# Where a graph kernel's adjacency is normalised: raw transposes with sums from their evacuations, against sums and scaling first

## The chip, the cores and the metric

The kernel runs on one core of one Trainium2 chip. The time is device microseconds of one execution, and each kernel is quoted by the median of its fast runs. Ratios are the mean time of one kernel's fast runs over that of the other's in the same rounds, so they are not quite the ratio of the medians quoted beside them. A difference under 2% is called "same".

## The reference, cut to what matters

```python
A_norm = A + jnp.eye(n)                                  # n = 1024
deg = jnp.sum(A_norm, axis=0) + jnp.sum(A_norm, axis=1) - jnp.diagonal(A_norm)
dinv = jax.lax.rsqrt(deg)
A_hat = A_norm * dinv[:, None] * dinv[None, :]
agg = jnp.einsum('nm,bmd->bnd', A_hat, features)         # 16 batches, d = 256
# then: linear, batch norm, relu, linear, batch norm, residual, layer norm,
# and a second layer with attention over 1024 nodes; none of that is changed
```

Everything after `agg` needs the normalised adjacency. It is computed once, at the start.

## The kernel before

All data is fp32. The adjacency arrives as four transfers of two row tiles each (a row tile is 128 rows by 1024). TensorE contracts over partitions, so the aggregation wants the adjacency transposed (`AhT`).

```python
            for i in range(NT):                                  # NT = 8 row tiles
                blk = A[i][:, ts(i, P)]
                nc.vector.tensor_add(blk, blk, ident)
                nc.vector.tensor_reduce(deg[:, i : i + 1], A[i], AX.X, OP.add)
                nc.vector.scalar_tensor_tensor(scr, blk, 1.0, ident, ..., accum_out=diag[:, i : i + 1])
            # [cut: W1 and W2 transposed on TensorE, evacuated by ScalarE]
            pd = ps.tile([P, FB], F32, tag="a", name="pd")
            for j in range(NT):
                for i in range(NT):                              # column sums: ones as moving operand
                    nc.tensor.matmul(pd[:, j : j + 1], A[i][:, ts(j, P)], ones, start=(i == 0), stop=(i == NT - 1))
            # [cut: deg = row sums + pd - diag; dinv = deg ** -0.5 on GpSimd]
            for i in range(NT):
                nc.vector.tensor_scalar_mul(A[i], A[i], dinv[:, i : i + 1])
            for j in range(NT):
                for h in range(NH):                              # NH = 2 halves of 512 nodes
                    p = ps.tile([P, FB], F32, tag="a", name="pat")
                    for k in range(FB // P):
                        nc.tensor.transpose(p[:, ts(k, P)], A[h * 4 + k][:, ts(j, P)], ident)
                    # [cut] evacuated times dinv of j, by VectorE (odd h) or ScalarE (even h)
```

In these traces each engine works in the order of the program text, on its own. In the aggregation one batch is four groups (two channel halves `c`, two node halves `h`) of eight accumulating matmuls. The trace shows every fp32 matmul as two records, so one batch is 64 records.

Of the kernel before, what the change touches and what calls it, by code (L numbers as in the profile page):

```python
# [9 lines left out]
F32 = mybir.dt.float32  # L10
AF = mybir.ActivationFunctionType
OP = mybir.AluOpType
AX = mybir.AxisListType
# [3 lines left out]
P = 128  # L17
# [5 lines left out]
def gnn_norm_attention_kernel(  # L23
# [16 lines left out]
    nc = tc.nc  # L40
    B, N, C = x.shape
    H = W1.shape[0]
    NT = N // P
    CT = C // P
    HT = H // P
    FB = 512
    NH = N // FB
# [7 lines left out]
    ident = const.tile([P, P], F32, name="ident")  # L55
    make_identity(nc, ident)
    ones = const.tile([P, 1], F32, name="ones")
# [4 lines left out]
    def rsqrt(dst, src, add):  # L62

        n = src.shape[1]
        if add:
            nc.gpsimd.tensor_scalar(dst, src, add, None, op0=OP.add)  # L66
            src = dst
        nc.gpsimd.tensor_tensor(dst, src, mhalf[:, :n], OP.pow)  # L68


    def load_vec(src, n, name):
        t = const.tile([P, n], F32, name=name)
        with nc.allow_non_contiguous_dma(reason="a few hundred numbers"):
            nc.sync.dma_start(t, src.rearrange("(c p) -> p c", p=P))
        return t
# [10 lines left out]
    with ExitStack() as l0:  # L86
        w0 = l0.enter_context(tc.tile_pool(name="w0", bufs=1))
# [28 lines left out]
        with ExitStack() as ph1:  # L116
            ahp = ph1.enter_context(tc.tile_pool(name="ahp", bufs=1))
            xp = ph1.enter_context(tc.tile_pool(name="xp", bufs=2))
            aggp = ph1.enter_context(tc.tile_pool(name="aggp", bufs=2))
            ps = ph1.enter_context(tc.tile_pool(name="ps1", bufs=4, space=PSUM))  # L120


            adj_r = adj.rearrange("(c p) m -> p c m", p=P)
            A = []
            for i in range(0, NT, 2):
                t = hp.tile([P, 2, N], F32, tag="h", name=f"A{i}")
                nc.sync.dma_start(t, adj_r[:, i : i + 2, :])
                A += [t[:, 0, :], t[:, 1, :]]
            xts = {}

            def load_x(b):
                if b < B:
                    xts[b] = xp.tile([P, NT, C], F32, tag="x", name=f"x{b}")
                    nc.sync.dma_start(xts[b], x[b].rearrange("(c p) d -> p c d", p=P))

            w1n = xp.tile([P, HT, C], F32, tag="w1n", bufs=1, name="w1n")
            nc.sync.dma_start(w1n, W1.rearrange("(c p) d -> p c d", p=P))
            w2n = xp.tile([P, CT, H], F32, tag="w2n", bufs=1, name="w2n")
            nc.sync.dma_start(w2n, W2.rearrange("(c p) d -> p c d", p=P))
            load_x(0)  # L140
            b1t, g1t, be1t = (load_vec(v, HT, n) for v, n in ((b1, "b1t"), (g1, "g1t"), (be1, "be1t")))
            b2t, g2t, be2t = (load_vec(v, CT, n) for v, n in ((b2, "b2t"), (g2, "g2t"), (be2, "be2t")))
            load_x(1)

            deg = w0.tile([P, NT], F32, name="deg")
            diag = w0.tile([P, NT], F32, name="diag")
            scr = w0.tile([P, P], F32, name="scr")
            for i in range(NT):
                blk = A[i][:, ts(i, P)]
                nc.vector.tensor_add(blk, blk, ident)  # L150
                nc.vector.tensor_reduce(deg[:, i : i + 1], A[i], AX.X, OP.add)
                nc.vector.scalar_tensor_tensor(
                    scr, blk, 1.0, ident, op0=OP.mult, op1=OP.mult, accum_out=diag[:, i : i + 1]
                )

            for c in range(HT):
                p = ps.tile([P, FB], F32, tag="a", name="pw1")
                for k in range(CT):
                    nc.tensor.transpose(p[:, ts(k, P)], w1n[:, c, ts(k, P)], ident)
                nc.scalar.copy(W1T[:, :, ts(c, P)], p[:, :C].rearrange("p (k f) -> p k f", k=CT))  # L160
            for c in range(CT):
                p = ps.tile([P, FB], F32, tag="a", name="pw2")
                for k in range(HT):
                    nc.tensor.transpose(p[:, ts(k, P)], w2n[:, c, ts(k, P)], ident)
                nc.scalar.copy(W2T[:, :, ts(c, P)], p.rearrange("p (k f) -> p k f", k=HT))

            pd = ps.tile([P, FB], F32, tag="a", name="pd")
            for j in range(NT):
                for i in range(NT):
                    nc.tensor.matmul(  # L170
                        pd[:, j : j + 1], A[i][:, ts(j, P)], ones, start=(i == 0), stop=(i == NT - 1)
                    )
            nc.vector.tensor_add(deg, deg, pd[:, :NT])
            nc.vector.tensor_sub(deg, deg, diag)
            dinv = w0.tile([P, NT], F32, name="dinv")
            rsqrt(dinv, deg, 0.0)

            AhT = ahp.tile([P, NT, N], F32, name="AhT")
            for i in range(NT):
                nc.vector.tensor_scalar_mul(A[i], A[i], dinv[:, i : i + 1])  # L180
            for j in range(NT):
                for h in range(NH):
                    p = ps.tile([P, FB], F32, tag="a", name="pat")
                    for k in range(FB // P):
                        i = h * (FB // P) + k
                        nc.tensor.transpose(p[:, ts(k, P)], A[i][:, ts(j, P)], ident)
                    if h % 2:
                        nc.vector.tensor_scalar_mul(AhT[:, j, ts(h, FB)], p, dinv[:, j : j + 1])
                    else:
                        nc.scalar.mul(AhT[:, j, ts(h, FB)], p, dinv[:, j : j + 1])  # L190


            def aggregate(b):
                aggT.append(aggp.tile([P, CT, N], F32, tag="agg", name=f"agg{b}"))
                for c in range(CT):
                    for h in range(NH):
                        p = ps.tile([P, FB], F32, tag="a", name="pa")
                        for k in range(NT):
                            nc.tensor.matmul(  # L199
                                p,  # L200
                                xts[b][:, k, ts(c, P)],
                                AhT[:, k, ts(h, FB)],
                                start=(k == 0),
                                stop=(k == NT - 1),
                            )
                        nc.scalar.copy(aggT[b][:, c, ts(h, FB)], p)  # L206
                load_x(b + 2)

            def hidden(b, h, f):
                p = ps.tile([P, FB], F32, tag="h", name="ph")  # L210
                for k in range(CT):
                    nc.tensor.matmul(  # L212
                        p,
                        W1T[:, k, ts(f, P)],
                        aggT[b][:, k, ts(h, FB)],
                        start=(k == 0),
                        stop=(k == CT - 1),
                    )
                return p

            for b in range(B + 1):
                if b < B:
                    aggregate(b)
                if b > 0:
                    for h in range(NH):
                        u = (b - 1) * NH + h
                        hT[u] = hp.tile([P, HT, FB], F32, tag="h", name=f"hT{u}")
                        for f in range(HT):
                            p = hidden(b - 1, h, f)
                            nc.scalar.copy(hT[u][:, f, :], p)  # L230
                            nc.vector.bn_stats(st1[:, f, u, :], p)  # L231
                            if u == len(units) - 1:
                                bn_affine(st1, f, g1t, be1t, b1t, s1, t1, "bn1")
                        if u < len(units) - KEEP:
                            nc.sync.dma_start(h_dram[u], hT.pop(u))
# [28 lines left out]
        with ExitStack() as ph2:  # L264
            yp = ph2.enter_context(tc.tile_pool(name="yp", bufs=3))
            ps = ph2.enter_context(tc.tile_pool(name="ps2", bufs=4, space=PSUM, reuse_waits="tile"))
# [530 lines left out]
```

## Time and profile before

Before: 2816.97 us, median of three runs (2816.69 to 2818.47).

| | before |
|---|---|
| span of the profiled run | 2816.4 us |
| TensorE busy | 98% |
| first aggregation matmul starts | 62.37 us |
| from there to the end of the span | 2754.0 us |

If TensorE is busy without a break from the first aggregation matmul to the end, a change to the prologue is worth exactly what it moves that start. The timeline of the kernel before gives the starts (columns: start us, duration us, engine and line, operation, tiles; then idle time before it and what ended it):

```profile
15.26 1.94 PE L159 MATMUL pw<-ident,w1n 128*128 128x128 f32 x8 [15.26 <-DMA w1n<-in_L_gnn_W_dram]
18.70 27.31 PE L170 MATMUL pd<-ones,A 128*128 128x1 f32 x128
```

TensorE does nothing for 15.26 us, until weights arrive that have nothing to do with the adjacency, and then spends 27.31 us on one-column matmuls.

### The profile page before, as it was taken

What the parts mean: (1) busy time and instruction counts of PE and PEld (TensorE: products, weight loads), DVE (VectorE), ACT (ScalarE), POOL (GpSimd) and SP (SyncE); (2) the same over time, 40 slices, a digit from 0 to 9 for tenths busy, and PEclk for the clock granted to TensorE, in tenths of its full rate; (3) what the DMA queues carried; (4) which work ended last, traced back from release to release, by engine and by line L of the source; (5) the groups of instructions that cost most, each with busy time, mean ns of one, the idle gap of its engine ahead of it and who ended that gap; (6) DMA issues with size and microseconds to landing.
All of it is one profiled execution on the core that took longest, in us unless ns stands there. A gap on an engine that the chain in (4) does not pass through costs nothing.

```text
span 2816.4 us, 26243 instructions
## 1 busy us (share of the span) xinstructions
PE 2750.9 (98%) x9426; PEld 1174.2 (42%) x9426; DVE 1352.6 (48%) x2364; ACT 1295.2 (46%) x1871; POOL 498.2 (18%) x660
## 2 busy tenths in 40 slices
PE   7999999999999899999999999999999999999998
PEld 6444444444444443434434434344343443434432
DVE  3011110111312456657666576575766756657556
ACT  1111111111555654646646556465564664655634
POOL 0000000000000113223122231232322313223113
PEclk9999999999999899999999999999999999999999
DMA  3121221130384200101001010010100100101000
GB/s 105 60 75 60 90 84 65 76 119 0 134 306 142 81 29 27 34 12 43 25 23 34 16 41 27 19 40 16 36 30 16 42 23 27 34 14 42 10 8 24
DMA packets 109993, 147.02 MB, mean 52 GB/s; under 512 B 10272, under 2 KB 92704, under 8 KB 103712
## 3 DMA queue, kind: packets, MB, share of 16 engines
q1 hardware_dynamic: 109856, 145.27, 15.0%
q8 instruction: 77, 1.26, 0.2%
q14 instruction: 60, 0.49, 0.1%
HBM read 86.52 MB, written 58.72 MB: 52 GB/s over the span
## 4 chain that ended last, share of the span: by engine, by line
PE 96%; DVE 2%; DMA 0%; ACT 0%; issue 0%; POOL 0%; SPq 0%; DVEq 0%; POOLq 0%; ACTq 0%
PE s L478 17%; PE o L508 17%; PE pg L458 16%; PE pa L199 16%; PE po L288 8%; PE ph L212 8%; PE pk L431 4%; PE pv L442 4%; PE pf L538 2%; PE pd L527 1%; PE py L371 1%; PE pd L170 1%; PE px L392 1%; PE pc L405 1%; PE pf L539 0%; DMA w1n<-in_L_gnn_W_dram 0%
## 5 line engine op out<-in xcount | busy, mean ns | idle before, releaser
L490 ACT ACTIVATE e<-s 128x1024 f32<-128x1024 f32 x512 | 496.4, 1022 | 409.2 <-PE s L478 408.7
L478 PE MATMUL s<-qT,kT 64*128 64x512 f32 x2048 | 508.8, 615 | 0.0
L508 PE MATMUL o<-e,v 128*64 128x512 f32 x2048 | 495.7, 605 | 0.0
L499 DVE TENSOR_TENSOR acc<-acc,e 128x1024 f32<-128x1024 f32 x384 | 466.9, 1216 | 41.5 <-ACT e L490 27.5
L458 PE MATMUL pg<-wg,x 128*128 128x512 f32 x1024 | 475.4, 602 | 1.5 <-DVE wg L423 1.3
L199 PE MATMUL pa<-AhT,x 128*128 128x512 f32 x1024 | 441.9, 592 | 0.0
L231 DVE BATCH_NORM_STATS2 st<-ph 128x6 f32<-128x512 f32 x128 | 89.4, 698 | 567.3 <-ACT hT L230 567.3
L478 PEld LDWEIGHTS s<-qT,kT 64*128 64x128 f32 x2048 | 176.2, 186 | 327.0 <-issue 244.8
L199 PEld LDWEIGHTS pa<-AhT,x 128*128 128x128 f32 x1024 | 194.5, 190 | 244.4 <-issue 244.2
L458 PEld LDWEIGHTS pg<-wg,x 128*128 128x128 f32 x1024 | 181.6, 190 | 240.5 <-issue 213.0
L423 DVE SCALAR_TENSOR_TENSOR wg<-wg,adj_sb 128x1024 f32<-128x1024 f32 x128 | 156.8, 1225 | 171.7 <-ACT wg L419 169.5
L206 ACT COPY agg<-pa 128x512 f32<-128x512 f32 x64 | 37.5, 586 | 402.3 <-PE pa L199 402.3
L212 PE MATMUL ph<-agg,W1T 128*128 128x512 f32 x512 | 222.2, 592 | 0.0
L508 PEld LDWEIGHTS o<-e,v 128*64 128x64 f32 x2048 | 124.2, 136 | 225.5 <-issue 212.6
L66 POOL TENSOR_SCALAR rs_z<-mv_z 128x1 f32<-128x1 f32 x128 | 52.2, 408 | 900.3 <-DVE mv_z L327 884.4
L66 POOL TENSOR_SCALAR rs_a<-mv_a 128x1 f32<-128x1 f32 x128 | 124.8, 975 | 435.8 <-DVE mv_a L327 435.7
L288 PE MATMUL po<-hL,W2T 128*128 128x512 f32 x384 | 165.0, 592 | 0.0
L68 POOL TENSOR_TENSOR rs_a<-rs_a,mhalf 128x1 f32<-128x1 f32 x128 | 157.9, 1234 | 10.7
L66 POOL TENSOR_SCALAR rs_bn<-mv_bn 128x1 f32<-128x1 f32 x6 | 1.3, 222 | 894.7 <-DVE mv_bn L104 894.7
L393 ACT COPY x1T<-px 128x256 f32<-128x256 f32 x128 | 47.7, 372 | 239.9 <-PE px L392 239.9
L212 PEld LDWEIGHTS ph<-agg,W1T 128*128 128x128 f32 x512 | 97.3, 190 | 122.5 <-issue 122.2
L230 ACT COPY hT<-ph 128x512 f32<-128x512 f32 x128 | 75.0, 586 | 144.7 <-PE ph L212 144.7
(101 smaller groups left out, 2540.7 us busy)
## 6 DMA issues: line engine op xcount, KB each, us to landing
h<-hT SPq DMA_DIRECT2D x24, 1024.0 KB, 3.8
hL<-h SPq DMA_DIRECT2D x24, 1024.0 KB, 6.4
x<-in_x_dram SPq DMA_DIRECT2D x16, 1024.0 KB, 5.4
yT<-y SPq DMA_DIRECT2D x32, 512.0 KB, 3.6
yt<-yT SPq DMA_DIRECT2D x128, 128.0 KB, 2.5
xr<-in_x_dram SPq DMA_DIRECT2D x128, 128.0 KB, 2.3
out_dram<-r SPq DMA_DIRECT2D x128, 128.0 KB, 1.7
A<-in_adj_dram SPq DMA_DIRECT2D x4, 1024.0 KB, 8.3
```

Source lines behind the costliest of these rows:

```text
L66: nc.gpsimd.tensor_scalar(dst, src, add, None, op0=OP.add)
L68: nc.gpsimd.tensor_tensor(dst, src, mhalf[:, :n], OP.pow)
L199: nc.tensor.matmul(p, xts[b][:, k, ts(c, P)], AhT[:, k, ts(h, FB)], start=(k == 0), stop=(k == NT - 1),)
L212: nc.tensor.matmul(p, W1T[:, k, ts(f, P)], aggT[b][:, k, ts(h, FB)], start=(k == 0), stop=(k == CT - 1),)
L288: nc.tensor.matmul(po[c], W2T[:, k, ts(c, P)], hT[u][:, k, :], start=(k == 0), stop=(k == HT - 1))
L423: nc.vector.scalar_tensor_tensor(t, t, 1.0, adj_sb[:, i, :], op0=OP.add, op1=OP.mult)
L431: nc.tensor.matmul(p, kvw[:, k, ts(c, P)], x1Ts[b][:, k, ts(h, FB)], start=(k == 0), stop=(k == CT - 1))
L458: nc.tensor.matmul(pg[b], x1s[b, k][:, ts(c, P)], wgs[b, k][:, ts(h, FB)], start=(k == 0), stop=(k == NT - 1))
L478: nc.tensor.matmul(t[:, h, :], kTs[b, pair][h * HD : (h + 1) * HD, ts(cb, P)], qTs[b, pair][h * HD : (h + 1) * HD, ts(hf, FB)], start=True ...
L490: nc.scalar.activation(E[g, a], S.pop((g, a)), AF.Exp)
L499: nc.vector.tensor_add(ACC[b, hf, pair], ACC[b, hf, pair], E[g, a])
L508: nc.tensor.matmul(O[b, hf, pair][h * HD : (h + 1) * HD, :], vs[b][:, cb, pair * P + h * HD : pair * P + (h + 1) * HD], E[g, a][:, h, :], ...
```

## The change

Its intent is to transpose the raw rows as soon as they land, take the column sums for nothing as accumulators of the PSUM evacuations, and apply both dinv factors to `AhT` in place, half by half, while the first half is already being used.

```diff
+            for h in range(NH):
+                rows = range(h * KB, (h + 1) * KB)
+                for i in rows:
+                    blk = A[i][:, ts(i, P)]
+                    nc.vector.tensor_add(blk, blk, ident)
+                    # [cut: diag[i] as before]
+                    if i % 2:
+                        nc.vector.tensor_reduce(row[:, i : i + 1], A[i], AX.X, OP.add)
+                    else:
+                        nc.scalar.activation(junk[:, 0, :], A[i], AF.Copy, accum_out=row[:, i : i + 1])
+                for j in range(NT):
+                    # [note: even j takes PSUM buffers "a", odd j PSUM buffers "h"]
+                    p = ps.tile([P, FB], F32, tag="ah"[j % 2], name="pat")
+                    for k, i in enumerate(rows):
+                        nc.tensor.transpose(p[:, ts(k, P)], A[i][:, ts(j, P)], ident)
+                    dst, acc = AhT[:, j, ts(h, FB)], col[:, h, j : j + 1]
+                    if j % 2:
+                        nc.vector.tensor_scalar(dst, p, 1.0, 0.0, op0=OP.mult, op1=OP.add, accum_out=acc)
+                    else:
+                        nc.scalar.activation(dst, p, AF.Copy, accum_out=acc)
+            # [cut: deg = row - diag + col[:, 0] + col[:, 1]; dinv on GpSimd]
+            def scale_half(h):
+                p = ps.tile([P, FB], F32, tag="h", name="pdr")
+                # [cut: four broadcast transposes of dinv into p]
+                for j in range(NT):
+                    t = AhT[:, j, ts(h, FB)]
+                    nc.vector.scalar_tensor_tensor(t, t, dinv[:, j : j + 1], p, op0=OP.mult, op1=OP.mult)
             # [cut: W1 and W2 transposed, unchanged, now after the adjacency]
-            # [cut: pd, the scaling of A[i], the scaled evacuations]
+            scale_half(0)
+            scale_half(1)
             # in aggregate(b):
-                for c in range(CT):
-                    for h in range(NH):
+                for h in range(NH):
+                    for c in range(CT):
```

The second load of x also moves ahead of the small bias vectors in the queue.

More of the change, by code (lines that the diff above doesn't have):

```diff
@@ L140, in gnn_norm_attention_kernel @@
             load_x(0)
+            load_x(1)
             b1t, g1t, be1t = (load_vec(v, HT, n) for v, n in ((b1, "b1t"), (g1, "g1t"), (be1, "be1t")))
             b2t, g2t, be2t = (load_vec(v, CT, n) for v, n in ((b2, "b2t"), (g2, "g2t"), (be2, "be2t")))
-            load_x(1)
-            deg = w0.tile([P, NT], F32, name="deg")
+            AhT = ahp.tile([P, NT, N], F32, name="AhT")
+            KB = FB // P
+            row = w0.tile([P, NT], F32, name="row")
+            col = w0.tile([P, NH, NT], F32, name="col")
@@ L146, in gnn_norm_attention_kernel @@
             diag = w0.tile([P, NT], F32, name="diag")
             scr = w0.tile([P, P], F32, name="scr")
-            for i in range(NT):
-                blk = A[i][:, ts(i, P)]
-                nc.vector.tensor_add(blk, blk, ident)
-                nc.vector.tensor_reduce(deg[:, i : i + 1], A[i], AX.X, OP.add)
-                nc.vector.scalar_tensor_tensor(
-                    scr, blk, 1.0, ident, op0=OP.mult, op1=OP.mult, accum_out=diag[:, i : i + 1]
-                )
+            junk = aggp.tile([P, CT, N], F32, tag="agg", name="junk")
@@ new lines, in gnn_norm_attention_kernel @@
+            for h in range(NH):
[3 more added lines that the diff above has]
+                    nc.vector.tensor_add(blk, blk, ident)
+                    nc.vector.scalar_tensor_tensor(
+                        scr, blk, 1.0, ident, op0=OP.mult, op1=OP.mult, accum_out=diag[:, i : i + 1]
+                    )
+                    if i % 2:
[11 more added lines that the diff above has]
+                        nc.scalar.activation(dst, p, AF.Copy, accum_out=acc)
@@ new lines, in gnn_norm_attention_kernel @@
+            deg = w0.tile([P, NT], F32, name="deg")
+            nc.vector.tensor_sub(deg, row, diag)
+            nc.vector.tensor_add(deg, deg, col[:, 0, :])
+            nc.vector.tensor_add(deg, deg, col[:, 1, :])
+            dinv = w0.tile([P, NT], F32, name="dinv")
+            rsqrt(dinv, deg, 0.0)
+            def scale_half(h):
+                p = ps.tile([P, FB], F32, tag="h", name="pdr")
+                for k in range(KB):
+                    i = h * KB + k
+                    nc.tensor.transpose(p[:, ts(k, P)], dinv[:, i : i + 1].to_broadcast([P, P]), ident)
+                for j in range(NT):
+                    t = AhT[:, j, ts(h, FB)]
+                    nc.vector.scalar_tensor_tensor(t, t, dinv[:, j : j + 1], p, op0=OP.mult, op1=OP.mult)
@@ L165, in gnn_norm_attention_kernel @@
                 nc.scalar.copy(W2T[:, :, ts(c, P)], p.rearrange("p (k f) -> p k f", k=HT))
-            pd = ps.tile([P, FB], F32, tag="a", name="pd")
-            for j in range(NT):
-                for i in range(NT):
-                    nc.tensor.matmul(
-                        pd[:, j : j + 1], A[i][:, ts(j, P)], ones, start=(i == 0), stop=(i == NT - 1)
-                    )
-            nc.vector.tensor_add(deg, deg, pd[:, :NT])
-            nc.vector.tensor_sub(deg, deg, diag)
-            dinv = w0.tile([P, NT], F32, name="dinv")
-            rsqrt(dinv, deg, 0.0)
-            AhT = ahp.tile([P, NT, N], F32, name="AhT")
-            for i in range(NT):
-                nc.vector.tensor_scalar_mul(A[i], A[i], dinv[:, i : i + 1])
-            for j in range(NT):
-                for h in range(NH):
-                    p = ps.tile([P, FB], F32, tag="a", name="pat")
-                    for k in range(FB // P):
-                        i = h * (FB // P) + k
-                        nc.tensor.transpose(p[:, ts(k, P)], A[i][:, ts(j, P)], ident)
-                    if h % 2:
-                        nc.vector.tensor_scalar_mul(AhT[:, j, ts(h, FB)], p, dinv[:, j : j + 1])
-                    else:
-                        nc.scalar.mul(AhT[:, j, ts(h, FB)], p, dinv[:, j : j + 1])
+            scale_half(0)
+            scale_half(1)
             def aggregate(b):
                 aggT.append(aggp.tile([P, CT, N], F32, tag="agg", name=f"agg{b}"))
-                for c in range(CT):
-                    for h in range(NH):
+                for h in range(NH):
+                    for c in range(CT):
                         p = ps.tile([P, FB], F32, tag="a", name="pa")
```

## The prediction

> **What bounds the kernel now.** I read the page's chain of waits first, then the same chain in order of time over the first 160 us, then the timeline and the groups of instructions of the first 63 us.
>
> ```profile
> PE 96%; DVE 2%; DMA 0%; ACT 0%; issue 0%; POOL 0%; SPq 0%; DVEq 0%; POOLq 0%; ACTq 0%
> ```
>
> TensorE is the chain that sets the end for 96% of the span. After the adjacency is ready it never stops for long (923.5 us busy of the 937.5 us from 62.5 to 1000 us). So anything that lets the first aggregation matmul start earlier shifts everything after it by as much. The chain in order of time shows what stands before it (start us, us, what):
>
> ```profile
> 3.01 12.11 DMA w1n<-in_L_gnn_W_dram
> ...
> 17.20 1.71 PE pw L164 x8
> 18.90 27.11 PE pd L170 x128
> ...
> 46.49 1.67 POOL dinv L68
> 48.18 5.40 DVE A L180 x8
> 53.59 0.04 issue
> 53.63 8.90 PE pat L186 x57
> 62.53 54.94 PE pa L199 x128
> ```
>
> The first pa matmul starts at 62.37 us in the timeline. Before it stand, in series: 15.1 us of waiting for the first-layer weights (queued behind the adjacency), 3.6 us of weight transposes, 27.1 us of column sums, 2.1 us for deg and its power, and 14.2 us of row scaling and transposing. The costs come from the groups of the first 63 us (busy us, mean ns of one, then idle before):
>
> ```profile
> L170 PE MATMUL pd<-ones,A 128*128 128x1 f32 x128 | 27.3, 351 | 0.0
> L151 DVE TENSOR_REDUCE deg<-A 128x1 f32<-128x1024 f32 x8 | 9.8, 1219 | 0.3
> L188 DVE TENSOR_SCALAR AhT<-pat,dinv 128x512 f32<-128x512 f32 x8 | 6.0, 751 | 3.7 <-PE pat L186 3.2
> L190 ACT ACTIVATE AhT<-pat,dinv 128x512 f32<-128x512 f32 x8 | 5.5, 688 | 37.8 <-PE pat L186 37.8
> L180 DVE TENSOR_SCALAR A<-A,dinv 128x1024 f32<-128x1024 f32 x8 | 5.4, 750 | 1.8 <-POOL dinv L68 1.8
> ```
>
> Column sums: 64 matmuls with one moving column, two records each, 27.3/128 = 0.213 us a record. A column of work costs as much as a weight load.
>
> Two windows inside the transposes, 57.6 to 58.4 us and 59.2 to 60.0 us, show one more thing:
>
> ```profile
> L186 PEld LDWEIGHTS pat<-ident,A 128*128 128x128 f32 x5 | 1.1, 230 | 0.0
> L186 PEld LDWEIGHTS pat<-ident,A 128*128 128x128 f32 x9 | 1.0, 141 | 0.0
> ```
>
> The weight load falls from 230 to 141 ns near 58.9 us. Evacuations come 1.71 us apart per engine before and 0.87 us after, so a transpose goes from 0.214 to 0.109 us. The granted clock reads 1.00 in both, so that column doesn't show it.
>
> **What the Trainium skill says.** "TensorE: Matmul & The Clock Gate", "What's actually happening": TensorE idles at half clock and is released after a busy window of about 3.4 us, at a phase of its own. The trace agrees in kind: dense transposes from 53.63 us, full speed near 58.9, 5.3 us later. The same page, "Part 4: PE-mode transpose", says that transposes do not engage the full clock; the trace differs, they double their rate, and I follow the trace. "VectorE: DVE Perf Modes", "Mode 2×_2P": single-source fp32 in SBUF runs two elements a cycle, a second tensor or a PSUM operand one. Agrees: 1024 elements from SBUF take 750 ns, 512 from PSUM 751. "ScalarE: Activation LUTs", "What ACT_TABLE_LOAD costs": with immediates 186 ns + 0.833 ns an element, 93 ns more for each per-partition operand. The trace has 688 ns with one such operand at 512 elements (formula 706), so the new plain copies should take about 0.6 us, and the row sums of 1024 about 1.04.
>
> **The change part by part.** Removed from the path: the wait for w1n ahead of any adjacency work, the 128 pd records (27.1 us), the row scaling pass of 5.4 us. Moved: transposing begins when rows arrive; the weight transposes stand after it, beside the degree work. Added: an accumulator on each evacuation, four row sums on ScalarE, 8 broadcast transposes of dinv, 16 in-place scalings on VectorE.
>
> Landing of the adjacency: issues at 0.73 to 2.25 us, 4.9 us (first) to 11.4 us (last) each, so 5.6 and 13.65; by the medians of subsets about 8.5 and 11.0 for the middle two.
>
> 1. VectorE, rows 0 to 3. A row took 1.665 us in the timeline (5.75 to 7.42), of which the reduce holds 1.13, so an even row is 0.53. Rows 0 and 1: 5.75 to 7.95. Rows 2 and 3, after the second landing at 8.5: until 10.7.
> 2. TensorE, first half: 32 transposes from 8.5. Cold, 0.214 x 4 = 0.86 a tile; released about 5 us later (13.7), then 0.44. The last tile is done near 15.
> 3. VectorE evacuates the four odd tiles as they come, 0.75 + 0.08 (the accumulator read, 84 ns in L152) = 0.83 each; the last ends near 15.6.
> 4. VectorE, rows 4 to 7, all behind it in program order: 2 x (0.53 + 1.665) = 4.4, until 20.0. TensorE has meanwhile done the second half's 32 transposes but for the last two tiles, which wait for the diagonal additions (about 18.6). ScalarE: row 6 until 19.2, four evacuations of about 0.7, until 22.
> 5. VectorE, second half's four evacuations, 4 x 0.83: until 23.3. **This engine sets the pace of the prologue, not the transposes.**
> 6. Three deg additions, 0.2 apart: 23.95. Power on GpSimd 1.66 plus 0.1 of handover: 25.75.
> 7. Four broadcast transposes, about 1.0 (cold): 26.75. First in-place scaling, 128x512 with a PSUM operand, 0.69 (qT from pg and para_sb) to 0.75: 27.5.
> 8. First aggregation matmul at 27.5 us. x has landed (4.86 + 15.0 = 19.9).
>
> From there VectorE delivers a scaled slice each 0.75 us. The aggregation takes 6.87 us for a group of 8 slices, 0.86 a slice. So it is not starved, and the second half is ready at 26.75 + 16 x 0.75 = 38.8, before its first reader at 27.5 + 2 x 6.87 = 41.2; that is what the swap of loops is for. But TensorE had only scattered weight transposes from about 19 to 25.7 us, so it probably starts cold: 3.4 to 6.8 us at half rate (5.3 was seen) loses 1.7 to 3.4, say 2.4.
>
> Sum: 62.4 - 27.5 - 2.4 = 32.5 us. 2817.0 - 32.5 = **2784.5 us**, 1.2% less. The swapped loops run the same number of matmuls; the earlier load of x1 only moves small vectors behind it, which nothing reads before the end of the first phase.
>
> **The rivals.**
> - *The in-place pass starves the aggregation.* If the scaling takes over 0.86 us (PSUM operand, broadcast and scalar in one instruction), the first group is paced by VectorE, and the second half comes late. For: no such instruction stands in the profile. Against: 128x512 forms from PSUM are all 0.69 to 0.75, and even 1.0 us would cost 8 x 0.14 plus 2 us: 2788.
> - *Accumulating evacuations are much dearer*, or their engines wait for one another (the row sums write one scratch area in turn). At 0.3 us more each, eight on VectorE give 2.4: 2787. Against: the one accumulator read there is takes 84 ns.
> - *The adjacency's arrival or cold transposes bound it.* Transposes cold throughout end at about 8.5 + 64 x 0.214 = 22.2, still before the VectorE evacuations end: under 1 us. The last landing, 13.65, precedes its use at about 15.6.
> - *TensorE stays warm.* The weight transposes may keep it so: 2782.
> - *The gain does not come through*, because a later stage is bound by something off TensorE. Against: the chain is TensorE from 62.53 us on with no transfer in it. I give it little: a few us.
>
> **Range and chances.** The uncertain terms are the half-clock loss (plus or minus 2), the VectorE chain (plus or minus 3) and unforeseen waits (up to 4 slower); the three runs of before lie within 1.8 us. So 2779 to 2791 eight times in ten. Faster by over 2% would need 56 us off, which leaves 6 us before the first matmul, about when the first quarter of the adjacency lands: nearly impossible. Slower by over 2% would need the swap or the buffers to hurt every batch; nothing points to it.
>
> **What would show it.** In the changed trace: no pd matmuls at the start; first transposes near 8.5 us; VectorE nearly without gaps from 8.5 to 23.3; dinv near 24; the first pa matmul near 27.5, its first few records at 0.86 us apart in place of 0.43; the steady stages of the same length. It is wrong if the first pa matmul comes after 33 us, if gaps stand between pa matmuls while they wait for AhT, or if the span after the first pa matmul differs from before (2754 us) by more than the half-clock loss.

## The result

The changed kernel takes 2782.23 us, median of four runs (2781.72 to 2782.44), against 2816.83 (2814.27 to 2818.47): ratio 0.9878, 95% interval 0.9861 to 0.9895. That is 34.6 us by the medians. The prediction was 2784.5, range 2779 to 2791.

The chain of waits of the changed kernel, as shares of the span:

```profile
PE 97%; DVE 2%; DMA 0%; issue 0%; POOL 0%; ACT 0%; SPq 0%; DVEq 0%; POOLq 0%; ACTq 0%
```

TensorE still sets the end. The same chain in order of time (start us, us, what):

```profile
1.24 6.94 DMA A<-in_adj_dram
...
8.22 5.17 PE pat L170 x30
...
13.42 0.70 DVE AhT L173 x2
...
15.20 1.13 DVE row L164
...
17.40 1.13 DVE row L164
...
19.05 1.91 DVE AhT L173 x7
...
21.60 1.67 POOL dinv L68
...
23.32 1.09 PE pdr L188 x8
...
24.94 56.87 PE pa L215 x128
```

The wait for w1n and the 27 us of pd are gone. The path goes from the second landing of rows to the transposes, and at 13.42 us to VectorE, which holds it until dinv: the diagonal work and row sums of rows 4 to 7, then the evacuations of the second half. The first aggregation matmul starts at 24.94 us, 37.4 us earlier. From there to the end are 2780.6 - 24.94 = 2755.7 us, 1.7 us more than before.

The weight loads of the first aggregation matmuls in the timeline of the changed kernel say what the 1.7 us are:

```profile
25.56 0.33 PEld L215 LDWEIGHTS pa<-AhT,x 128*128 128x128 f32 x1 [0.35 <-DVE AhT L191]
26.41 0.33 PEld L215 LDWEIGHTS pa<-AhT,x 128*128 128x128 f32 x1 [0.52 <-issue]
27.27 0.33 PEld L215 LDWEIGHTS pa<-AhT,x 128*128 128x128 f32 x1 [0.52 <-DVE AhT L191]
28.12 0.33 PEld L215 LDWEIGHTS pa<-AhT,x 128*128 128x128 f32 x1 [0.52 <-issue]
28.86 0.19 PEld L215 LDWEIGHTS pa<-AhT,x 128*128 128x128 f32 x1 [0.41 <-DVE AhT L191]
29.29 0.19 PEld L215 LDWEIGHTS pa<-AhT,x 128*128 128x128 f32 x1 [0.24 <-issue]
```

They come 0.86 us apart until 28.1 and 0.43 us apart from 28.9, and one load shortens from 0.33 to 0.19 us. "DVE AhT", named as releaser in these lines, is not the cause: it is the latest event known, but VectorE delivers slices every 0.66 us (16 scalings in 10.62 us) and a slice lasts two records, so it is well ahead of a TensorE that takes 1.71 us for one. The granted clock, which is the share of full TensorE clock that the trace records, is the cause. In windows of 2 us (window, us, TensorE's busy time with its records, granted clock, share of the DMA engines, GB/s) it reads:

```profile
24.00:26.00 2.00, 1.47 (x6) 0.83 0.01 4
26.00:28.00 2.00, 2.00 (x3) 0.50 0.03 8
28.00:30.00 2.00, 2.00 (x5) 0.81 0.00 0
```

In finer windows it is 0.50 from 25.33 to 28.74 us and 1.00 on both sides. Half speed for 3.41 us loses 1.7 us, which is the whole difference.

Last, the groups of the changed kernel's first 45 us:

```profile
L191 DVE SCALAR_TENSOR_TENSOR AhT<-AhT,dinv,pdr 128x512 f32<-128x512 f32 x16 | 10.6, 741 | 2.6 <-PE pdr L188 2.6
L173 DVE TENSOR_SCALAR_CACHE_REDUCE AhT<-pat 128x512 f32<-128x512 f32 x8 | 5.3, 686 | 0.9 <-PE pat L170 0.9
L175 ACT ACTIVATE AhT<-pat 128x512 f32<-128x512 f32 x8 | 4.7, 592 | 1.3 <-PE pat L170 1.3
L175 ACT ACTIVATION_READ_ACCUMULATOR AhT<-pat 128x1 f32 x8 | 1.6, 198 | 0.0
```

The evacuation with an accumulator takes 686 ns on VectorE, no more than the scaled one of before (751). The accumulator reads are separate, short instructions.

### The profile page after: what moved, and what is told of

Same layout as the page of the kernel before. It is cut to its first block, busy times and chain, and to the rows that moved or that the text cites. A ratio compares the mean times of both kernels' runs of the same rounds, so it can differ in the third digit from the quotient of the medians.

```text
span 2780.6 us, 26036 instructions
## 1 busy us (share of the span) xinstructions
PE 2724.5 (98%) x9306; PEld 1145.7 (41%) x9306; DVE 1353.0 (49%) x2377; ACT 1297.7 (47%) x1887; POOL 498.1 (18%) x660
## 3 DMA queue, kind: packets, MB, share of 16 engines
HBM read 86.52 MB, written 58.72 MB: 52 GB/s over the span
## 4 chain that ended last, share of the span: by engine, by line
PE 97%; DVE 2%; DMA 0%; issue 0%; POOL 0%; ACT 0%; SPq 0%; DVEq 0%; POOLq 0%; ACTq 0%
PE s L494 18%; PE o L524 17%; PE pg L474 16%; PE pa L215 16%; PE po L304 8%; PE ph L228 8%; PE pk L447 4%; PE pv L458 4%; PE pf L554 2%; PE pd L543 1%; PE py L387 1%; PE px L408 1%; PE pc L421 1%; PE pf L555 0%; DVE qT L479 0%
## 5 line engine op out<-in xcount | busy, mean ns | idle before, releaser
L515 DVE TENSOR_TENSOR acc<-acc,e 128x1024 f32<-128x1024 f32 x384 | 467.0, 1216 | 41.9 <-ACT e L506 27.5
L68 POOL TENSOR_TENSOR rs_a<-rs_a,mhalf 128x1 f32<-128x1 f32 x128 | 157.9, 1234 | 10.7
```

The costliest lines, as they stand in the source:

```text
L68: nc.gpsimd.tensor_tensor(dst, src, mhalf[:, :n], OP.pow)
L515: nc.vector.tensor_add(ACC[b, hf, pair], ACC[b, hf, pair], E[g, a])
```

## The experiments

All kernels gave correct results. The theory: the gain is the earlier start of the aggregation and nothing else. Most of it comes from taking the column sums off TensorE, a smaller part from starting before the weights come, and what remains of the prologue is paced by VectorE and by TensorE's half clock. The rivals: the reordering alone carries it; the swap of loops carries it; the slow first aggregation matmuls wait for data and not for the clock.

The changed kernel itself ran again as a yardstick.

> The changed kernel unaltered, as the yardstick for the runs beside it: 2782 us, 34 to 35 us under the kernel before; first aggregation matmul near 24.9 us.

Measured: 2782.41 us (2781.96 to 2783.49); the kernel before beside it 2816.82 (2813.39 to 2818.16). The kernel before falls into two groups, 2813 to 2815 us (mean granted clock 0.989) and 2817 to 2818 (0.995); why the shorter group has the lower clock is open. One reading, which no trace shows because the profiled run is of the longer group: a trace's clock record begins with the first release to full clock, at 58.72 us in that run, and 1.00 is printed before it for want of a record, although its transposes ran at half rate until then. Runs released earlier, and back at half clock for the column sums, would be quicker and yet record more half clock. So small differences are read against the yardstick and not against it.

> The changed kernel unaltered, beside the next three on one chip: 2782 us. Where TensorE's clock windows fall differs from run to run: the first 30 transposes of the chain took 4.9 to 6.2 us in the runs so far, the first 128 aggregation records 55.2 or 56.9.

Measured: 2782.48 us (2781.46 to 2782.91).

### The column sums put back on TensorE

```diff
-                        nc.vector.tensor_scalar(dst, p, 1.0, 0.0, op0=OP.mult, op1=OP.add, accum_out=acc)
+                        nc.vector.tensor_scalar(dst, p, 1.0, 0.0, op0=OP.mult, op1=OP.add)
                     # [cut: the same on ScalarE]
+            # after all transposes: the pd loop of the kernel before, on the raw rows
-            nc.vector.tensor_add(deg, deg, col[:, 0, :])
-            nc.vector.tensor_add(deg, deg, col[:, 1, :])
+            nc.vector.tensor_add(deg, deg, pd[:, :NT])
```

> The changed kernel with the column sums made by TensorE again (64 one-column matmuls on the raw rows, after the transposes, before the weight transposes) and no accumulators on the evacuations. My theory (the column sums on TensorE were most of the gain): 128 records of 0.213 us stand on the path again from 17.5 us, first aggregation matmul near 49 us, 2806 us. Rival (starting the transposes with the rows gave the gain, and the sums would hide beside other work): under 10 us over the changed kernel. Second rival (coming after dense transposes, they run at full clock, 0.11 to 0.14 us a record): near 2794 us.

Measured: 2804.82 us (two runs at 2803.0, two near 2806.7), 22.4 us over the yardstick beside it. The first theory holds and the first rival falls; the second holds for the first 3.5 us of pd only, as shown below. The first aggregation matmul starts at 47.40 us. But it came 1 us under my figure. The weight loads of pd in two windows of this kernel, 19.3 to 20.3 us and 22.3 to 23.3 us, say why:

```profile
L179 PEld LDWEIGHTS pd<-ones,A 128*128 128x128 f32 x10 | 1.2, 192 | 0.0
L179 PEld LDWEIGHTS pd<-ones,A 128*128 128x128 f32 x6 | 1.4, 333 | 0.0
```

In one microsecond there are ten of them first, then six, 3 to 4 us into the pd work. After dense transposes the one-column matmuls start at full clock, and then the clock falls to half although the record shows TensorE busy all the time: the granted clock reads 1.00 until 21.81 us and 0.50 from there to 45.70. The loads stay slow (333 ns again at 30 us). So the 27 us of pd in the kernel before were half-clock microseconds: such work does not hold the clock.

### The weight transposes put back in front

```diff
+            # [the W1 and W2 transposes, moved back]
             for h in range(NH):
                 rows = range(h * KB, (h + 1) * KB)
```

> The changed kernel with the weight transposes put back in front of the adjacency's transposes, so that TensorE waits again for the weights behind the adjacency in the queue. My theory: the first adjacency transpose moves from 8.2 to about 18.9 us and VectorE's evacuations with it, first aggregation matmul near 35 us, 2792 us. Rival (VectorE is the pace and does not care when the transposes come): within 3 us of the changed kernel.

Measured: 2791.67 us (2790.82 to 2792.89), 9.3 us over the yardstick. First adjacency transposes at 18.3 us in the chain, first aggregation matmul at 34.00. The theory holds.

### The reordering alone, on the kernel before

```diff
-            # [the W1 and W2 transposes]
             pd = ps.tile([P, FB], F32, tag="a", name="pd")
             # [cut: the pd loop]
+            # [the W1 and W2 transposes]
```

> The kernel before with one thing of the change: the weight transposes moved behind the column sums. The sums can then start when the last rows land (13.65 us) and not at 18.9, and the weight transposes stand partly beside deg and its power: about 5 us under the kernel before, 2812 us. If the reordering alone carried the gain it would be 15 us or more.

Measured: 2810.01 us (2809.60 to 2810.28) against 2815.15 for the kernel before, 5.1 us less by the medians. The first aggregation matmul moves from 62.37 to 54.59 us in the profiled runs; that is 7.8, as the profiled run of the kernel before is one of its longer group. 12 of the 128 pd records already ran while rows were arriving, which I had not counted. Reordering alone does not carry the gain.

### The old order of loops and of the second load

```diff
-                for h in range(NH):
-                    for c in range(CT):
+                for c in range(CT):
+                    for h in range(NH):
             # and load_x(1) behind the small vectors again
```

> The changed kernel with the aggregation's loops back in the old order (channel half outside, node half inside) and the second x load back behind the small vectors. From the trace, slices of the second half are ready from about 30 us, one each 0.66 us, and the old order would ask for the first at about 33.7 us: so 0 plus or minus 0.5 us. Rival (my prediction's reason for the swap): TensorE waits for the second half in the second group, 1 to 5 us slower.

Measured: 2781.61 us (2781.30 to 2782.18), if anything 0.8 us under the yardstick (2781.96 to 2783.49). The rival falls: neither edit is needed here. Slices are ready long before the second group asks, in either order. In the profiled run of this kernel the clock also happened to be full at the start of the aggregation (128 records in 55.17 us, and not 56.87), with every TensorE instruction ahead of it the same. So the cold start isn't caused by the program text alone.

### Keeping TensorE busy in the wait for dinv: first attempt

```diff
+            keep_busy(6)     # needless transposes of A into an unread PSUM tile with the tag "h"
             # [cut: the weight transposes]
+            keep_busy(14)
             scale_half(0)
```

> The changed kernel with 20 needless transposes into an unread PSUM tile, 6 before and 14 after the weight transposes, in the time in which TensorE waits for dinv. My theory (the first five aggregation records take 0.86 us because TensorE fell to half clock while it waited): they take 0.43 us, and the time falls by about 1.9 us. Rival (they wait for VectorE's scaled slices, or the first use is slow for another reason): no gain, 0 to 0.5 us slower.

Measured: 2782.42 us (2780.56 to 2783.90), no gain against the first yardstick's 2782.41. The profile shows two effects that cancel. The chain in order of time:

```profile
20.11 1.38 PE dum L197 x6
21.49 1.71 PE pw L203 x8
23.20 1.20 PE pw L208 x8
24.40 1.53 PE dum L197 x14
25.93 0.87 PE pdr L188 x8
26.80 0.54 issue
27.34 55.17 PE pa L222 x128
```

The aggregation starts at full clock (55.17), so the slow records were the clock and not data. But the filler itself is now on the path: the first six wait for a PSUM buffer that VectorE still holds, and pdr comes at 25.93, while dinv is done at 22.52 + 1.66 = 24.2.

### Second attempt: filler only after the weight transposes

```diff
             # [cut: the weight transposes]
+            keep_busy(12)
             scale_half(0)
```

> The changed kernel with 12 needless transposes after the weight transposes only, where their PSUM buffer is long free, since in the first attempt those before the weight transposes waited for VectorE's evacuation and delayed everything by 1.6 us. My theory: no aggregation records at 0.86 us, first aggregation matmul not later than 0.3 us after its time in the changed kernel: 0.5 to 1.9 us off, by how often the changed kernel starts cold. Rival: no gain, as in the first attempt.

Measured: 2782.86 us (2781.59 to 2783.70) against 2782.48 for the yardstick beside it: no gain, my theory's figure missed. The profiled run started the aggregation at full clock (55.17), but only at 26.29 us. Its first half's transposes took 5.96 us, the weight transposes ran at half clock, and the filler ended 0.7 us after dinv. So the cold start is real, and removing it this way isn't worth anything.

The traces together show why it can't be had so simply. The clock was released in the first half, and where it was released early it was down again when the aggregation began. Five profiled runs have the same TensorE work before the aggregation (the last moves one row sum between other engines, see below):

| unaltered TensorE work before the aggregation | first 30 transposes | clock released at | next half clock | first 128 aggregation records |
|---|---|---|---|---|
| changed kernel, first yardstick | 4.92 us | 11.22 us | 24.88 to 28.29 us | 56.87 us |
| changed kernel, its first run | 5.17 us | 11.67 us | 25.33 to 28.74 us | 56.87 us |
| changed kernel, second yardstick | 5.33 us | 12.06 us | not before 900 us | 55.17 us |
| old order of loops | 5.51 us | 12.48 us | not before 900 us | 55.17 us |
| one row sum moved | 6.20 us | 13.86 us | 20.69 to 24.10 us | 55.17 us |

In the last of them the slow stretch fell on the weight transposes, ahead of the aggregation; so it did in this kernel (20.20 to 23.62 us) and in the first attempt (20.33 to 23.75). One slow stretch is exchanged for another. The clock records show why it is a matter of the run: in all fourteen traces every stretch of one clock, but for the last, which the end of the span cuts, is a whole multiple of 3.41 us (3.41, 6.83, 10.24, 13.65, 17.07 us and more). So in these runs the clock changes only at the edges of windows of that length, and where the edges lie differs from run to run. What in a window decides the next is not shown.

### TensorE warmed before the first rows come

```diff
+            p = ps.tile([P, FB], F32, tag="h", name="pre")
+            for k in range(32):
+                nc.tensor.transpose(p[:, ts(k % KB, P)], ident, ident)
             for h in range(NH):
                 rows = range(h * KB, (h + 1) * KB)
```

> The changed kernel with 32 needless transposes of the identity into an unread PSUM tile while TensorE waits for the first rows. My theory (the first half's transposes start at half clock, and VectorE waits for them): they run at 0.11 us from the start, the first half's evacuations are then bound by VectorE, dinv and the first aggregation matmul come 1 to 2 us earlier: 1 to 2 us off. Rival (VectorE's own program is the pace there as well, or the clock falls again before the rows come): within 0.5 us.

Measured: 2780.98 us (2779.67 to 2781.53), 1.5 us under the yardstick: the theory holds. The chain of waits:

```profile
9.37 1.13 DVE row L168
10.50 2.44 DVE AhT L177 x8
...
20.41 1.67 POOL dinv L68
...
23.75 56.72 PE pa L219 x128
```

The transposes have left the path (32 of them in 3.71 us), and VectorE evacuates four tiles without a gap, 2.44 us, 0.61 each. dinv starts at 20.41 and not at 21.60. The aggregation then starts cold again: the half clock lasts from 23.45 to 26.86 us.

### One row sum moved to ScalarE

```diff
-                    if i % 2:
+                    if i % 2 and i != 5:
                         nc.vector.tensor_reduce(row[:, i : i + 1], A[i], AX.X, OP.add)
```

> The changed kernel with the row sum of row tile 5 moved from VectorE to ScalarE, which sits idle for 1.05 us there. My theory (VectorE's program order sets when dinv is ready): dinv and the first aggregation matmul come about 1.0 us earlier, 1.0 us off the time. Rival (ScalarE's evacuations or the transposes set it): no gain, or up to 1 us slower. It may also change whether TensorE starts cold, worth up to 2 us either way.

Measured: 2779.65 us (2779.27 to 2781.40), 2.8 us under the yardstick's median of the other two calls (2782.41 and 2782.48), more than the 1.0 of the row sum. The profiled run is the longest of its four and doesn't show the rest. In it the first half ended 1.1 us later than in the changed kernel (14.50 against 13.40, by the clock), and dinv started at 21.61 against 21.60: the 1.1 us were made up behind it, as expected. But dinv no longer sets the start there: it was done at 23.3, while TensorE, behind ScalarE's evacuations, was at the weight transposes until 23.78, part of them at half clock. Why the other three runs gained 2.7 to 3.2 us stays open; a kinder meeting with the clock would do it, but no trace of those runs exists.

> Both edits at once, with 6 and 10 needless transposes. If the two are separate costs they add: about 2.9 us under the changed kernel, the fastest of all. If the earlier dinv alone keeps TensorE warm, they add to less.

Measured: 2780.50 us (2779.65 to 2781.19). The edits do not add: the filler of the first attempt costs what it brings. The profiled run has the full clock at the aggregation (55.17 from 25.14).

### Filler in both places and the row sum moved

> Both fillers and the row sum of tile 5 on ScalarE. If the three costs are separate: 3 to 4 us under the changed kernel, 2778 to 2779 us, and less spread over its runs. If they overlap, or ScalarE becomes the bound: 1 to 2 us.

Measured: 2779.47 us (2778.87 to 2779.72), 3.0 us under the yardstick beside it (2781.46 to 2782.91; the ranges don't touch), and the smallest spread of all. The chain of waits:

```profile
16.87 2.32 ACT AhT L179 x8
...
21.90 0.87 PE pdr L192 x8
22.77 0.54 issue
23.31 55.17 PE pa L225 x128
```

The aggregation starts at 23.31 us at full clock. ScalarE's evacuations are now on the path, so VectorE is no longer alone in setting it. The second filler holds the start up too: dinv was done at 21.1, pdr began at 21.90. It is the fastest version, but the row sum moved alone is within 0.2 us of it; the fillers add little that these runs can show.

## Why the prediction was right

**The mechanism.** The gain is the shift of the first aggregation matmul. In the nine profiled runs of this table the rest of the span hardly varies:

| kernel | first aggregation matmul, us | span minus that, us | first 128 records, us |
|---|---|---|---|
| before | 62.37 | 2754.0 | 55.1 |
| reordering alone | 54.59 | 2753.8 | 55.1 |
| column sums back | 47.40 | 2753.8 | 55.17 |
| weights in front | 34.00 | 2755.2 | 55.98 |
| old loops | 25.39 | 2754.3 | 55.17 |
| changed, second yardstick | 25.15 | 2754.6 | 55.17 |
| changed | 24.94 | 2755.7 | 56.87 |
| prewarmed | 23.75 | 2755.9 | 56.72 |
| all three | 23.31 | 2754.3 | 55.17 |

The start moves over 39 us and the rest within 2.1; where it is longest, the first 128 records are slow. (The five other profiled runs lie between 2753.2 and 2755.8.) The rival that the gain does not come through is out.

**What it is made of.** By single undoings: 22.4 us for the column sums, 9.3 for not waiting for the weights, 31.7 together of 34.4 (2816.82 - 2782.41). The rest is not taken apart; it holds the separate row scaling (5.4 us in the chain of before) less what the in-place scaling costs ahead of the first matmul, and the meetings with the clock.

**Step by step.** Step 1, rows 0 to 3 on VectorE until 10.7: 10.42. Step 4, 4.4 us for rows 4 to 7: 14.04 to 18.45, 4.41. Step 6, deg and power, 2.45 us: 20.89 to 23.28, 2.39. Step 7, from dinv to the first matmul 1.75: 1.66. ScalarE's plain evacuations, which I had estimated at about 0.6 us, took 592 ns, and its row sums, estimated at 1.04 us, took 1057 ns. These were right, and so was the claim that VectorE sets the pace, for the second half; in the first half it waited for transposes, as the prewarmed kernel showed.

Two terms were mis-sized, which is why the start came at 24.94 and not at 27.5:

- *Step 5 (and 3), "4 x 0.83".* I added the duration of an evacuation and of its accumulator read. The four took 18.45 to 20.89, 0.61 each: consecutive VectorE instructions overlap, so a duration is not a pitch. The error is 0.9 us. The timeline of before had shown it: a row took 1.665 us, less than the sum of its instructions' durations.
- *Step 2, "Released about 5 us later".* The first half's tiles were done at 13.4, not near 15. I took one earlier release, which I put 5.3 us after dense transposes began (the clock record of before has it at 58.72 us, 5.1 after), for the rule, with a landing 0.3 us too late. In this run the clock was released at 11.67 us, 3.5 us after the start of the chain's 30 transposes, and two of the 32 had run before it. My own figures also give about 14.5 for the last tile (six of 0.86 us and two of 0.44 from 8.5), which I rounded up. The first half's evacuations ended at 14.04 and not near 15.6: 1.6 us. Other runs drew otherwise: with the same text ahead of them the 30 transposes took 4.9 to 6.2 us.

**The half-clock loss**, predicted 2.4, measured 1.7 (56.87 - 55.17) in two of the three profiled runs of the changed kernel and zero in the third. It is one window of 3.41 us at half rate, the low end of the 3.4 to 6.8 us that I allowed. The same sum fits the two other slow starts: the half clock covered the first 1.64 us of the aggregation with the weights in front and 3.11 us in the prewarmed kernel, and their 128 records took 0.81 and 1.55 us longer. I wrote that the column of the granted clock doesn't show such a thing; that is so in the trace of before, whose record begins with the release at 58.72 us, but in the changed kernel's trace it does. The sum for the profiled run: 62.4 - 24.9 - 1.7 = 35.8, the difference of the two spans. By medians it is 34.6, as the profiled run of the kernel before is in its longer group.

**The swap of loops.** The prediction said that the swap is what gets the second half ready in time ("that is what the swap of loops is for"). That was wrong. With the old order the first slice of the second half is asked for about 6.9 us after the first matmul, and VectorE has delivered the whole first half 5.3 us after it began. The run shows no loss.

**The rivals.** In-place scaling above 0.86 us: it took 0.66. Dear accumulators: VectorE's read 82 ns, ScalarE's 198, no more. Cold transposes: not for the whole, but for the first half they cost 1.5 us. TensorE stays warm: sometimes. That rival's 2782 us is next to the measured median, but that is luck: the profiled run started cold and was as fast because the aggregation began 2.5 us before my figure.

## What to carry to other kernels

When one engine is busy from its first useful instruction to the end, a change to the prologue is worth exactly the shift of that instruction; find it in the timeline and subtract. Take reductions from passes that have to be made anyway, rather than give a matrix engine one column at a time, and let nothing stand ahead of the data that the path needs first. For chains of short instructions, count the spacing of starts in the trace and not the durations, and before filling a wait with needless work, check that the filler's own buffer is free.

## What the Trainium skill lacked or had wrong

- "TensorE: Matmul & The Clock Gate", "Part 4: PE-mode transpose", says that transposes do not engage the full clock. They do here: the weight load of a transpose fell from 230 to 141 ns within a run of transposes, and 32 needless transposes before the data came let the first half run in 3.71 us.
- The same page, "Busy/warm" in "What's actually happening", does not say that one-column matmuls leave the clock at half. Here 128 records of them, without a gap, stayed at 333 ns a weight load for 27 us, and let a full clock fall after 3.5 us.
- No page that I found gives the cost of ScalarE's accumulator read, which is an instruction of its own: 187 to 198 ns, though starts are only 0.57 us apart for a 592 ns evacuation with its read.
